# A four-layer graph network on one core: fused maximum, scores through HBM, and a first adjacency matrix turned by TensorE

## The chip, the core and the metric

The kernel runs on one core of a Trainium2 chip. The metric is the device time of one launch, in microseconds (us). A core has engines that work side by side, each through its own queue in order: TensorE (PE in the profile) multiplies matrices and turns 128x128 blocks, and writes to PSUM, eight banks of 128x512 float32; VectorE (DVE) and ScalarE (ACT) work on elements and read PSUM; GpSimd (POOL) works on SBUF; SyncE (SP) issues most of the loads. All data are float32.

## The reference

There are 16 graphs of 1024 nodes with 128 features: x is 16x1024x128, adj is 16x1024x1024 of weights, most of them zero. Four layers follow one another, each on `h = max(layernorm(x), 0)` and added to x:

```python
# layer 0, three times: h = h @ W + b; nh = h / norm(h)
cos = einsum('bij,bkj->bik', nh, nh);  h = einsum('bpq,bqc->bpc', adj * cos, h)
# layer 1
y = maximum((x + einsum('bnf,bnm->bmf', x, adj)) @ W1 + b1, 0) @ W2 + b2
# layer 2: h = x @ W; s1 = h @ a[:f]; s2 = h @ a[f:]
attn = softmax(where(adj > 0, tanh(s1[:, :, None] + s2[:, None, :]), -1e15), -1) @ h
# layer 3: h = x @ W.T + b; e = (h @ A) @ h.T; e = e + e.T
att = softmax(where(adj > 0, e, 0), axis=1) * adj;  h_prime = relu(att @ h)
# then three gates of [x, h_prime], sigmoid and tanh
```

In layer 3 the softmax needs a maximum over 1024 entries for each of the 1024 columns. In layer 2 one score of every node, s1, has to stand in a row that all 128 partitions can read.

## The kernel before

One graph after the other is computed. A graph's nodes are eight blocks of 128; a matrix of 1024x1024 is worked on in eight chunks of 128 rows, each in two halves of 512 columns (`HALVES`). The helpers `pe`, `act`, `dve`, `pool_op` and `op` only record operations, with an estimated duration, the tiles read and written, and a function that emits the instructions. When all 16 graphs are recorded, `Plan.order` (L137) simulates the engines and picks an order: among the operations of the engine that could start first, within `WINDOW`, it takes the one with the lowest rank, which is the graph's due time (`PERIOD` per graph, L345) less the estimated work that still follows it, less an adjustment from the table `LEADS` (L347). The keys of the table name layer, engine and tile; suffixes such as `<0` and `>1` stand for the first two and the last two graphs. `POOLS` and `KINDS` (L338, L339) say how many buffers there are of each kind and how many of them a younger graph may hold. Two further graphs may be under way (`AHEAD`). The instructions are emitted in this order with a manual schedule, so each queue is fixed.

What the change and the prediction touch:

- `load` (L844) loads x of a graph, 512 KB as one DMA on SP's queue; for graph 0 it is two halves. The constants go through `load_const` (L276): the first weights w0 and b0 on ACT's queue, all others on POOL's.
- `turn` (L866) brings the turned adj of a graph, eight tiles adjT of 128x1024. For each there are four DMAs (L879) that put 32x32 squares in their places, in pieces of 32 floats; a 32x32 transpose by DVE (L887) turns the squares, and ACT (L890) copies the tile onto itself to sum its rows (su).
- `layernorm` (L660): statistics on DVE, a power on POOL (L562), then scaling, one half by DVE (L698) and one by ACT (L705). `flipped` (L626) turns the result with TensorE (L569) and evicts it with ACT (`evict`, L622).
- `layer0` (L895): for each chunk, `Square.row` (L748) makes the symmetric product sq: only the upper blocks are multiplied (L760). In most graphs the lower quarter comes back by way of HBM (by_hbm, got), and the rest is turned from copies above (L770, L792). DVE multiplies by adjT (L959) and TensorE accumulates (L822, L833).
- `layer1` loads adj once more, unturned (adjL), and accumulates it with L822.
- `layer2` (L1028): after the projection h, each block's column of scores is widened to 128 columns and turned by TensorE, which leaves the scores in every partition (L1090, eight transposes to a graph); two evictions make s1. Then ACT takes tanh (L1101) and exp (L1105) of each chunk, DVE masks (L1109), TensorE accumulates.
- `layer3` (L1136): for each chunk, DVE masks two halves of the product from PSUM with `adjT > 0` (L1177) into e, reduces 1024 columns to the negated maximum top (L1189); ACT takes exp with that bias and sums (L1193); DVE multiplies by adjT (L1202), and TensorE accumulates.
- The gates follow in `finish` (L1252), and z is stored from ACT's queue.

The heart of layer 3's chunk before the change:

```python
lambda ...: nc.vector.scalar_tensor_tensor(
    by_block(span(e.t, lo, hi), D, 4), by_block(span(aT[j].t, lo, hi), D, 4), 0.0, view(),
    op0=ALU.is_gt, op1=ALU.mult,
),
...
lambda e=e, top=top: nc.vector.tensor_reduce(top.t, e.t[:, 0:N], axis=AX.X, op=ALU.max, negate=True),
```

Of the kernel before, what the change touches and what calls it, by code (L numbers as in the profile page):

```python
# [9 lines left out]
U8 = mybir.dt.uint8  # L10
AF = mybir.ActivationFunctionType
# [3 lines left out]
P = 128  # L15
# [8 lines left out]
FLOOR = 1e-30  # L24

# [197 lines left out]
def tile_adj_preln(  # L223
# [40 lines left out]
    FLAGS = set("CabcdkxhyzTG")  # L264
# [11 lines left out]
    def load_const(group, t, src):  # L276
        def emit():
            with nc.allow_non_contiguous_dma(reason="small parameters, once"):
                (nc.gpsimd if "G" in FLAGS and group is not first else nc.scalar).dma_start(t, src)

        group.append(emit)
# [44 lines left out]
    for load_it in first:  # L326
# [11 lines left out]
    POOLS = {"adjT": 16, "adjL": 5, "x": 3, "big": 13, "above": 2, "got": 1, "bank": 8, "small": 29, "row": 6, "hbm": 3, "hrow": 2}  # L338
    KINDS = {  # L339
        "adjT": ("adjT", 16, 16), "adjL": ("adjL", 5, 5), "x": ("x", 3, 3), "w4": ("big", 12, 8),  # L340
        "chunk": ("big", 11, 4), "above": ("above", 2, 1), "got": ("got", 1, 1), "ps": ("bank", 5, 5),
        "acc": ("bank", 8, 6), "small": ("small", 7, 6), "row": ("row", 3, 3), "hbm": ("hbm", 3, 2),
        "hrow": ("hrow", 2, 1),
    }
    PERIOD, LAST, AHEAD, WINDOW = 60.0, 52.0, 2, 0.05  # L345

    LEADS = {  # L347
        "0 ACT hT": -1, "0 DVE hn": -8, "0 DVE mv": 42.5, "0 DVE nb": -20, "0 DVE st": -77.5, "0 PE ps": -72.5,
        "0 POOL rstd": -1, "00 ACT above": -10.5, "00 ACT hT": 95, "00 ACT hTn": -20.5, "00 ACT sq": -31,
        "00 DMA by": -13.5, "00 DMA got": 15.5, "00 DVE above": -135, "00 DVE ew": 79.5, "00 DVE h": -95.5,  # L350
        "00 DVE ss": -131.5, "00 PE acc0": -252.5, "00 PE ps": -142, "00 PE psP": -0.5, "00 PE sq": -18.5,
        "00 POOL rn": -129.5, "01 ACT above": 56, "01 ACT hT": 11.5, "01 ACT hTn": 15, "01 ACT sq": 15.5,
        "01 DMA by": 4.5, "01 DMA got": 18.5, "01 DVE above": 4.5, "01 DVE ew": 51.5, "01 DVE h": -2.5,
        "01 DVE ss": 16, "01 PE acc0": -164.5, "01 PE ps": 42, "01 PE psP": -5.5, "01 PE sq": -11,
        "02 ACT above": -2, "02 ACT hTn": -615, "02 ACT sq": -25.5, "02 DMA by": 63.5, "02 DMA got": 0.5,
        "02 DVE above": 43.5, "02 DVE ew": -232.5, "02 DVE ss": 79.5, "02 DVE x": -55.5, "02 PE acc0": -28.5,
        "02 PE ps": 12.5, "02 PE sq": 222, "02 POOL rn": -103, "1 ACT g": -33, "1 ACT hn": 66, "1 ACT y1": -7.5,
        "1 DMA adjL": -113, "1 DVE adjL": -21, "1 DVE hn": 1.5, "1 DVE mv": 237.5, "1 DVE nb": 46,
        "1 DVE st": -625.5, "1 DVE x": -0.5, "1 PE acc1": 4, "1 PE py": -167.5, "1 PE py2": 67,
        "1 POOL rstd": -43, "2 ACT e2": -24, "2 ACT h": 287.5, "2 ACT hfl": 53, "2 ACT hn": -13.5,  # L360
        "2 ACT hnT": 18, "2 ACT s1": -14, "2 DVE alone": -51.5, "2 DVE e2": 48.5, "2 DVE h": 20,
        "2 DVE hn": 48.5, "2 DVE hrow": -43.5, "2 DVE mv": -2.5, "2 DVE nb": 78, "2 DVE rden": 9.5,
        "2 DVE x": 10, "2 PE acc2": 108.5, "2 PE p1": -90, "2 PE pf": -26.5, "2 PE ps": 117.5, "2 PE psP": -315,
        "2 POOL rstd": 4.5, "3 ACT above": -19.5, "3 ACT e3": 96.5, "3 ACT gate": -185.5, "3 ACT h3T": 19.5,
        "3 ACT hn": -84.5, "3 ACT hnT": -9.5, "3 ACT hp": -5, "3 ACT hpT": 41, "3 ACT hs": 46.5, "3 ACT z": 25,
        "3 DMA by": -13.5, "3 DMA got": 0.5, "3 DMA z": -130.5, "3 DVE e3": -363.5, "3 DVE gate": 83,
        "3 DVE h": -111.5, "3 DVE hn": 69, "3 DVE mv": -2, "3 DVE nb": 147, "3 DVE st": -192, "3 DVE sum": 53.5,
        "3 DVE top": -84, "3 DVE z": -925, "3 PE acc3": -130.5, "3 PE pg": -18.5, "3 PE ps": 19,
        "3 PE psN": 114, "3 PE psP": 95, "3 PE sq": -0.5, "3 POOL rstd": -59, "3 POOL z": 0.5,
        "T ACT adjT": 1.5, "T DMA adjT": -140.5, "T DVE adjT": -391, "x DMA x": 54.5, "0 ACT hT <0": -2,  # L370
        "0 ACT hT >1": -4.5, "0 ACT hn <1": -4.5, "0 DVE hn <0": 8.5, "0 DVE hn <1": 8.5, "0 DVE hn >0": 15.5,
        "0 DVE hn >1": 1, "0 DVE mv <0": -4.5, "0 DVE mv <1": 113, "0 DVE mv >0": 47.5, "0 DVE mv >1": -25.5,
        "0 DVE nb <0": 101.5, "0 DVE nb <1": -62.5, "0 DVE nb >0": -49, "0 DVE nb >1": -18.5,
        "0 DVE st <0": -85, "0 DVE st <1": -73.5, "0 DVE st >0": -122.5, "0 DVE st >1": -32, "0 PE ps <0": 85.5,
        "0 PE ps <1": 36, "0 PE ps >0": -31, "0 PE ps >1": 40, "0 POOL rstd <0": -6.5, "0 POOL rstd <1": -26,
        "0 POOL rstd >0": -7, "0 POOL rstd >1": 15.5, "00 ACT above <0": -32, "00 ACT above <1": -88,
        "00 ACT above >0": -294, "00 ACT above >1": -3, "00 ACT hT <0": 147.5, "00 ACT hT <1": -7,
        "00 ACT hT >0": 21, "00 ACT hT >1": 161.5, "00 ACT hTn <0": -70.5, "00 ACT hTn <1": 119.5,
        "00 ACT hTn >0": -22, "00 ACT hTn >1": -11, "00 ACT sq <0": -34, "00 ACT sq <1": 134.5,
        "00 ACT sq >0": -119, "00 ACT sq >1": -25.5, "00 DMA by <1": 0, "00 DMA got <1": 1,  # L380
        "00 DVE above <1": -197, "00 DVE ew <0": 180, "00 DVE ew <1": 13, "00 DVE ew >0": -125,
        "00 DVE ew >1": -147.5, "00 DVE h <0": -25.5, "00 DVE h <1": -4.5, "00 DVE h >0": 12,
        "00 DVE h >1": -50.5, "00 DVE params <0": 171, "00 DVE ss <0": 0, "00 DVE ss <1": -73.5,
        "00 DVE ss >0": -46.5, "00 DVE ss >1": -4, "00 PE acc0 <0": -39.5, "00 PE acc0 <1": -212,
        "00 PE acc0 >0": -327.5, "00 PE acc0 >1": -253.5, "00 PE params <0": 56.5, "00 PE ps <0": -18.5,
        "00 PE ps <1": -16, "00 PE ps >0": -32, "00 PE ps >1": -130.5, "00 PE psP <0": -2.5, "00 PE psP <1": 32,
        "00 PE psP >0": -22.5, "00 PE psP >1": -43, "00 PE sq <0": 28.5, "00 PE sq <1": 10, "00 PE sq >0": 3.5,
        "00 PE sq >1": 10, "00 POOL rn <0": -11, "00 POOL rn <1": -164.5, "00 POOL rn >0": -96.5,
        "00 POOL rn >1": -144, "01 ACT above <0": 113, "01 ACT above <1": -11, "01 ACT above >0": 65.5,
        "01 ACT above >1": 24, "01 ACT hT <0": -15, "01 ACT hT <1": -17.5, "01 ACT hT >0": 3.5,  # L390
        "01 ACT hT >1": -39, "01 ACT hTn <0": 16.5, "01 ACT hTn <1": -22, "01 ACT hTn >0": 68,
# [111 lines left out]
    def small(name, n):  # L503
        return Buf("small", [P, n], name)
# [930 lines left out]
```

## Time and profile before

| What | Value |
|---|---|
| median of three runs | 2436.25 us (2435.44 to 2436.89) |
| span of the profiled execution | 2432.9 us |
| granted TensorE clock, mean | 0.996 |
| instructions | 34859 |
| DMA | 263.35 MB, mean 108 GB/s |
| masking in layer 3 from sq, L1177 | 204 of 672 ns; 52 more from got, 681 ns |
| maximum in layer 3, L1189 | 128 of 1212 ns |
| exp with sum in layer 3, L1193 | 128 of 1149 ns, and 187 ns to read the sum |
| score transposes, L1090 | 128 of 273 ns each as recorded |
| stream transposes of adjT, L887 | 128 of 1224 ns |
| copies of adjT with sum, L890 | 128 of 1055 ns, and 190 ns to read the sum |

A page of the profile gives, for one execution, each engine's busy time; then 40 equal slices of the span with busy tenths; then groups of instructions. A group's line names the source line, engine and operation, what it writes and reads, and the tile shapes; then the number of instructions, the busy time with the mean duration of one in ns, and the engine's idle time before them with what ended it. Matmuls are pipelined: a recorded duration holds the way through the array, and what one costs in a stream is read from the distance of the starts. A float32 matmul is recorded as two instructions, a transpose as one.

The idle time of an engine is told by windows of time (busy us of each engine in each stretch), and the timeline shows instructions in order, with the idle time in front and what ended it.

### The profile page before, as it was taken

The numbers are of one execution on the slowest core, as the hardware profiler recorded it, in microseconds if no ns is written. First come the engines' busy times: TensorE is split into PE (matmuls) and PEld (weight loads), VectorE is DVE, ScalarE is ACT, GpSimd is POOL, SyncE is SP. The second block draws the span as 40 slices with busy tenths as digits, with TensorE's granted clock in tenths as the row PEclk, the third lists the DMA queues.
The fourth block names the chain that finished last, engine by engine and source line by source line (L and its number), as shares of the span: only waits on it lengthen the run. The fifth ranks groups of instructions, "written<-read, shape, count | busy, mean of one in ns | idle before, by whom it ended". The sixth has DMA issues, their size and how long they took to land. (4 is left out here: it accounts for less than half of the span.)

```text
span 2432.9 us, 34859 instructions
## 1 busy us (share of the span) xinstructions
PE 2387.8 (98%) x11946; PEld 1589.5 (65%) x11946; DVE 2107.7 (87%) x5264; ACT 1288.8 (53%) x2404; POOL 245.1 (10%) x166
## 2 busy tenths in 40 slices
PE   6999999999999999999999999999999999999996
PEld 3568576675767657676675767757576675765763
DVE  6758989889998988999888998998999888897676
ACT  5316564645646465554744646455454644656275
POOL 3001010100101101010010101001011010100011
PEclk9999999999999999999999999999999999999998
DMA  9531927549295573936639285473936738063000
GB/s 149 111 104 36 173 53 148 130 88 171 62 165 121 103 155 81 166 86 136 142 80 180 53 164 130 92 151 80 165 103 122 155 75 151 18 94 89 27 1 18
DMA packets 1126321, 263.35 MB, mean 108 GB/s; under 512 B 970016, under 2 KB 1109552, under 8 KB 1126144
## 3 DMA queue, kind: packets, MB, share of 16 engines
q1 hardware_dynamic: 1108368, 251.73, 52.9%
q10 hardware_dynamic: 16944, 8.52, 1.2%
q8 instruction: 94, 1.54, 0.3%
q0 software_dynamic: 832, 0.88, 0.3%
q14 instruction: 83, 0.68, 0.1%
HBM read 198.14 MB, written 62.91 MB: 107 GB/s over the span
## 5 line engine op out<-in xcount | busy, mean ns | idle before, releaser
L959 DVE SCALAR_TENSOR_TENSOR ew<-sq,rn,adjT 128x512 f32<-128x512 f32 x612 | 432.3, 739 | 83.3 <-ACT above L792 45.6
L822 PE MATMUL acc<-ew,h 128*128 128x512 f32 x1024 | 477.9, 593 | 2.1 <-DVE ew L959 2.1
L760 PE MATMUL sq<-hTn 128*128 128x512 f32 (+3 forms) x1152 | 432.8, 488 | 0.7 <-DVE above L782 0.4
L792 ACT COPY above<-sq 128x256 f32<-128x256 f32 (+3 forms) x432 | 168.2, 394 | 448.5 <-PE sq L760 248.7
L760 PEld LDWEIGHTS sq<-hTn 128*128 128x128 f32 x1152 | 201.4, 192 | 155.2 <-issue 103.9
L822 PEld LDWEIGHTS acc<-ew,h 128*128 128x128 f32 x1024 | 178.9, 190 | 161.8 <-issue 124.0
L833 PEld LDWEIGHTS acc<-h,ew 128*128 128x128 f32 x2048 | 240.8, 192 | 22.6 <-issue 18.8
L833 PE MATMUL acc<-h,ew 128*128 128x128 f32 x2048 | 250.3, 276 | 0.0
L822 PE MATMUL acc<-e,hs 128*128 128x512 f32 x512 | 242.1, 597 | 5.3 <-DVE e L1202 4.1
L833 PEld LDWEIGHTS acc<-h,e 128*128 128x128 f32 x2048 | 232.9, 192 | 11.9 <-issue 6.5
L833 PE MATMUL acc<-h,e 128*128 128x129 f32 x2048 | 233.8, 275 | 1.2 <-DVE e L1109 1.2
L822 PE MATMUL acc<-adjL,hn 128*128 128x512 f32 x512 | 233.5, 593 | 0.3 <-ACT hn L726 0.3
L562 POOL TENSOR_TENSOR rstd<-ve,mhalf 128x8 f32<-128x8 f32 x64 | 105.2, 1643 | 1237.1 <-DVE ve L681 1237.1
L1193 ACT ACTIVATE e<-e,top 128x1024 f32<-128x1024 f32 x128 | 147.0, 1149 | 133.8 <-DVE top L1189 131.8
L770 PEld LDWEIGHTS sq<-ident,above 128*128 128x128 f32 x960 | 125.7, 141 | 125.6 <-issue 89.0
L890 ACT ACTIVATE adjT<-adjT 128x1024 f32<-128x1024 f32 x128 | 135.0, 1055 | 137.2 <-DVE adjT L887 94.5
L770 PE MATMUL sq<-ident,above 128*128 128x128 f32 x960 | 175.1, 273 | 2.0 <-ACT above L792 2.0
L705 ACT ACTIVATE hn<-x,nb,rstd 128x128 f32<-128x128 f32 x256 | 105.3, 482 | 122.8 <-DVE nb L689 115.2
L1109 DVE SCALAR_TENSOR_TENSOR e<-adjT,e 128x512 f32<-128x512 f32 x256 | 158.8, 681 | 9.3 <-ACT e L1105 8.7
L887 DVE STREAM_TRANSPOSE adjT<-adjT 128x1024 f32<-128x1024 f32 x128 | 154.7, 1224 | 11.7 <-DMA adjT<-in_adj_dram 11.0
L782 DVE STREAM_TRANSPOSE above<-sq 128x512 f32<-128x512 f32 x208 | 146.5, 707 | 17.2 <-PE sq L760 17.1
L1202 DVE TENSOR_TENSOR e<-e,adjT 128x512 f32<-128x512 f32 x248 | 161.2, 681 | 0.0
(149 smaller groups left out, 3512.0 us busy)
## 6 DMA issues: line engine op xcount, KB each, us to landing
adjT<-in_adj_dram SPq DMA_DIRECT2D x512, 128.0 KB, 4.0
adjL<-in_adj_dram SPq DMA_DIRECT2D x128, 512.0 KB, 5.0
by_hbm<-above SPq DMA_DIRECT2D x104, 512.0 KB, 3.7
got<-by_hbm SPq DMA_DIRECT2D x416, 128.0 KB, 3.0
x<-in_x_dram SPq DMA_DIRECT2D x15, 512.0 KB, 4.6
out_dram<-z ACTq DMA_DIRECT2D x15, 512.0 KB, 5.6
x<-in_x_dram SPq DMA_DIRECT2D x2, 256.0 KB, 4.9
out_dram<-z ACTq DMA_DIRECT2D x2, 256.0 KB, 2.2
```

What stands on the lines that cost most here:

```text
L760: lambda: nc.tensor.matmul(dst.t[:, (first - lo) * P :], cols(leftT.t, j), span(rightT.t, first, hi), start=True, stop=True),
L770: nc.tensor.transpose(cols(dst.t, r), cols(above.t, p), ident)
L782: lambda: nc.vector.transpose(span(above.t, p, p + 4), read.t),
L792: lambda: nc.scalar.copy(span(above.t, p, p + hi - first), read.t[:, (first - lo) * P :]),
L822: lambda s=s, lo=lo, hi=hi: nc.tensor.matmul(acc[s].t, cols(h.t, at, w), span(ew.t, lo, hi), start=(j == 0), stop=(j == NB - 1)),
L833: nc.tensor.matmul(a.t[:, (c - lo) * n : (c - lo + 1) * n], cols(ew.t, c), h.t[:, at * w : at * w + n], start=(j == 0 and c == lo), stop=( ...
L887: dve(V(N), [t], [t], lambda t=t: nc.vector.transpose(t.t, t.t), True)
L890: lambda t=t, c=c: nc.scalar.activation(t.t, t.t, AF.Copy, accum_out=su.t[:, c : c + 1]),
L959: lambda view=view, ew=ew, rn=rn, j=j, lo=lo, hi=hi: nc.vector.scalar_tensor_tensor(by_block(span(ew.t, lo, hi), D, 4), view(), rn.t[:, j ...
L1109: lambda e=e, j=j, lo=lo, hi=hi: nc.vector.scalar_tensor_tensor(span(e.t, lo, hi), span(aT[j].t, lo, hi), 0.0, span(e.t, lo, hi), op0=ALU. ...
L1193: lambda e=e, top=top, tot=tot: nc.scalar.activation(e.t[:, 0:N], e.t[:, 0:N], AF.Exp, bias=top.t, accum_out=tot.t),
L1202: lambda e=e, j=j, lo=lo, hi=hi: nc.vector.tensor_mul(span(e.t, lo, hi), span(e.t, lo, hi), span(aT[j].t, lo, hi)),
```

## The change

Four flags are switched on, and the plan's tables are replaced.

- `m`: in layer 3, ACT makes a mask of 0 and 1 in int8 from each adjT tile by Sign and then Relu, in one of five new buffers. DVE multiplies the mask by the product and takes the maximum of the half in the same instruction; a small reduction joins the two maxima and negates.
- `r`: in layer 2 of every graph but the last, one transpose turns the 128x8 scores into 8x128, ACT evicts it, a DMA writes it to HBM, and a second DMA reads it back into all 128 partitions as s1. The last graph keeps the eight transposes.
- `H`: for graph 0, adj comes in eight blocks of 128 columns (pieces of 512 bytes, buffers of kind adjL); TensorE turns them, eight transposes to a block, and ACT evicts the halves with their sums.
- `W`: the second half of x of graph 0, and x of graphs 1 and 2, are issued on ACT's queue, the latter two after the second eviction of graph 0's first hT; from graph 2 on, the loads of x are kept in order; all constants are loaded from POOL's queue.
- `POOLS`, `KINDS`, `PERIOD`, `LAST` and every entry of `LEADS` are new, so all queues are ordered anew. The top and sum columns get a pool of their own, `dot`.

```diff
-    FLAGS = set("CabcdkxhyzTG")
+    FLAGS = set("CabcdkxhyzTGmrHW")
...
-                (nc.gpsimd if "G" in FLAGS and group is not first else nc.scalar).dma_start(t, src)
+                (nc.gpsimd if "W" in FLAGS or "G" in FLAGS and group is not first else nc.scalar).dma_start(t, src)
...
-        "adjT": ("adjT", 16, 16), "adjL": ("adjL", 5, 5), "x": ("x", 3, 3), "w4": ("big", 12, 8),
-        "chunk": ("big", 11, 4), "above": ("above", 2, 1), "got": ("got", 1, 1), "ps": ("bank", 5, 5),
-        "acc": ("bank", 8, 6), "small": ("small", 7, 6), "row": ("row", 3, 3), "hbm": ("hbm", 3, 2),
-        "hrow": ("hrow", 2, 1),
+        "adjT": ("adjT", 16, 16), "adjL": ("adjL", 5, 5), "x": ("x", 3, 3), "w4": ("big", 9, 10),
+        "chunk": ("big", 11, 4), "above": ("above", 2, 1), "got": ("got", 1, 1), "ps": ("bank", 6, 8),
+        "acc": ("bank", 8, 8), "small": ("small", 8, 9), "row": ("row", 3, 2), "hbm": ("hbm", 3, 3),
+        "hrow": ("hrow", 1, 2), "mask": ("mask", 5, 5), "dot": ("dot", 8, 5),
     }
-    PERIOD, LAST, AHEAD, WINDOW = 60.0, 52.0, 2, 0.05
+    PERIOD, LAST, AHEAD, WINDOW = 59, 45.5, 2, 0.05
...
         for lo, hi in HALVES if "x" in FLAGS and b == 0 else ((0, NB),):
+            queue = nc.scalar if "W" in FLAGS and (b == 0 and lo or b in (1, 2)) else nc.sync
...
+            if "W" in FLAGS and b > 1:
+                plan.place_after(o, loads["x"])
+            loads["x"] = o
+            if "W" in FLAGS and b in (1, 2):
+                plan.place_after(o, [p for p in plan.ops if p.key == "0 ACT hT"][1])
+                o.preds.add([p for p in plan.ops if p.key == "0 ACT hT"][1])
...
+        for c in range(NB) if sh else ():
+            t = Buf("adjT", [P, N], f"adjT_{b}_{c}")
+            raw = Buf("adjL", [P, N], f"raw_{b}_{c}")
+
+            def plain(raw=raw, c=c):
+                nc.sync.dma_start(by_block(raw.t), adj[b].rearrange("(a p) j -> p a j", p=P)[:, :, c * P : (c + 1) * P])
+
+            o = op("DMA", 1.9, [], [raw], plain)
...
+            for s, (lo, hi) in enumerate(HALVES):
+                p = ps(f"raw_{b}_{c}_{s}")
+                flip(raw, lo, hi, p)
+                evict(p, t, lo, hi, accum=(sh, 2 * c + s))
...
+        if "r" in FLAGS and b < B - 1:
+            pt, sr = ps(f"pt_{b}"), rowbuf(f"sr_{b}")
+            pe(
+                TR, [h], [pt],
+                lambda: nc.tensor.transpose(pt.t[0:NB, 0:P], by_block(h.t, E2)[:, :, D], ident),
+            )
+            act(S(P), [pt], [sr], lambda: nc.scalar.copy(sr.t[0:NB], pt.t[0:NB, 0:P]))
+            sd = Buf("hrow", [NB, P], f"sd_{b}")
+            op("DMA", 0.2, [sr], [sd], lambda: nc.sync.dma_start(sd.t, sr.t[0:NB]), lat=2.2)
+            op(
+                "DMA", 1.8, [sd], [s1],
+                lambda: nc.sync.dma_start(s1.t[:, 0:N], sd.t.rearrange("c p -> (c p)").partition_broadcast(P)),
+                lat=2.4,
+            )
...
+            if "m" in FLAGS:
+                mask = Buf("mask", [P, N], f"mask_{b}_{j}")
+                act(
+                    S(N), [aT[j]], [mask],
+                    lambda mask=mask, j=j: nc.scalar.activation(mask.t, aT[j].t, AF.Sign),
+                )
+                act(S(N), [mask], [mask], lambda mask=mask: nc.scalar.activation(mask.t, mask.t, AF.Relu))
+                peak = dot(f"peak_{b}_{j}", 2)
...
+                if "m" in FLAGS:
+                    dve(
+                        V(HALF) + 0.06, [blk(mask, lo, hi), p], [blk(e, lo, hi), blk(peak, s, s + 1, 1)],
+                        lambda e=e, view=view, mask=mask, peak=peak, s=s, lo=lo, hi=hi: nc.vector.tensor_tensor_reduce(
+                            by_block(span(e.t, lo, hi), D, 4), by_block(span(mask.t, lo, hi), D, 4), view(), 1.0, LOWEST,
+                            op0=ALU.mult, op1=ALU.max, accum_out=peak.t[:, s : s + 1],
+                        ),
+                        p is square.got,
+                    )
...
-            top = small(f"top_{b}_{j}", 1)
-            tot = small(f"sum_{b}_{j}", 1)
-            dve(
+            tot = dot(f"sum_{b}_{j}", 1)
+            if "m" in FLAGS:
+                dve(
+                    TINY, [peak], [top],
+                    lambda peak=peak, top=top: nc.vector.tensor_reduce(
+                        top.t, peak.t, axis=AX.X, op=ALU.max, negate=True
+                    ),
+                )
```

## The prediction, made before the changed kernel was run

> **What bounds the kernel now.** I read the busy shares first, then the slices, then the windows, because a share over the whole span hides where the idle time lies.
>
> ```profile
> PE 2387.8 (98%) x11946; PEld 1589.5 (65%) x11946; DVE 2107.7 (87%) x5264; ACT 1288.8 (53%) x2404; POOL 245.1 (10%) x166
> ```
> ```profile
> PE   6999999999999999999999999999999999999996
> DVE  6758989889998988999888998998999888897676
> ACT  5316564645646465554744646455454644656275
> ```
> ```profile
> 0.00:60.00 60.00, 39.82 (x158) 23.88 (x159) 39.66 (x106) 30.16 (x60) 23.11 (x36) 0.95 1.10 149
> ...
> 500.00:650.00 150.00, 150.00 (x740) 98.76 (x739) 134.31 (x339) 77.79 (x145) 13.36 (x8) 1.00 0.61 120
> ...
> 2300.00:2433.00 133.00, 110.56 (x512) 69.54 (x510) 97.69 (x268) 80.88 (x151) 25.12 (x12) 0.95 0.07 20
> ```
>
> In the windows the columns after the length are PE, weight loads, DVE, ACT and POOL busy, then clock, DMA share and GB/s. TensorE is idle for 2432.9 - 2387.8 = 45.1 us, and 20.2 of them lie in the first 60 us, 22.4 in the last 133. Between, it never rests, at clock 1.00. A busy TensorE need not be a full one, so I checked its spacing in the timeline of TensorE alone:
>
> ```profile
> 2300.46 11.32 PE L822 MATMUL acc<-adjL,hn 128*128 128x512 f32 x26
> 2311.62 0.60 PE L569 MATMUL ps_hnT<-ident,hn 128*128 128x128 f32 x4
> ...
> 2338.20 0.60 PE L1090 MATMUL p<-ident,h 128*128 128x128 f32 x4
> 2338.64 1.04 PE L770 MATMUL sq<-ident,above 128*128 128x128 f32 x8
> ```
>
> 26 matmuls start in 2311.62 - 2300.46 = 11.16 us, 0.429 us each, and that is also the usual spacing elsewhere: the stream has no bubbles. Four transposes take 0.44 us, 0.110 each. So in the middle only less work on TensorE buys time. DVE (134.3 of 150 us) and ACT (77.8) follow it; relief on DVE buys nothing there. At the two ends other things decide:
>
> ```profile
> 2.34 38.50 SPq L879 DMA_DIRECT2D adjT<-in_adj_dram  x32
> ...
> 7.82 0.87 DVE L670 BATCH_NORM_STATS2 st<-x 128x6 f32<-128x128 f32 x4 [2.85 <-DMA x<-in_x_dram]
> ...
> 12.53 2.01 PE L569 MATMUL ps_hT<-ident,hn 128*128 128x128 f32 x8 [12.53 <-DVE hn L698]
> ...
> 40.42 1.25 DVE L887 STREAM_TRANSPOSE adjT<-adjT 128x1024 f32<-128x1024 f32 x1 [2.40 <-DMA adjT<-in_adj_dram]
> ```
> ```profile
> 2390.64 1.13 DVE top L1189
> 2391.77 1.19 DVE e L1177 x2
> 2392.96 1.13 DVE top L1189
> 2394.16 1.18 DVE e L1177 x2
> 2395.34 1.13 DVE top L1189
> ```
>
> At the start, TensorE waits 12.5 us for the first layer norm, whose second half of x comes at 7.8, and the first graph's turned adj trickles in until 44.5 us (32 DMAs, 38.5 / 32 = 1.2 us apart). At the end the chain of waits alternates on DVE between masking and the maximum of layer 3.
>
> **What the Trainium skill says.** "TensorE: Matmul & The Clock Gate", Part 1: after about 3.4 us of idleness the array falls to half clock. The trace agrees: after the 4.9 us of idleness before 55.65 us, the clock over 56 to 62 us is 0.56. "ScalarE: Activation LUTs", Table sets: cheap functions ride in every set, and another set costs about 2.66 us. The trace has one table load (1283 ns) although exp, tanh, relu and square alternate; the page does not list Sign for this set. "VectorE: DVE Perf Modes", Two Vector instructions with no wait between them: an op that writes its accumulator is two instructions, the second reading it out. No DVE op here has one; ACT's read-out takes 187 ns. "DMA: Bandwidth & Descriptors", Issuing engines are not separate DMA queues: a second issuing queue saves issue time alone.
>
> **The change part by part.** Durations are of the profiled execution, whose span is 2432.9 us; the median 2436.25 is 3.4 above it. I apply the difference to the median.
>
> *Scores through HBM.* For graphs 0 to 14, eight transposes (L1090) become one: 15 x 7 x 0.110 = 11.5 us off TensorE, in its saturated stretch: worth 11.5 us. Two evictions into s1 (618 ns) become one of 128 columns (about 270 ns as hfl, L1067). In exchange two DMAs on SP's queue. The nearest rows are by_hbm (3.7 us to landing) and got (3.0), so the first tanh of layer 2 comes some 6 us later than by transposes. While it does, TensorE has other graphs' matmuls, since two batches ahead may run. If that cover failed, each graph would lose up to 6 us, 15 x 6 = 90; I take 0. On SP the write waits for the eviction, and adjT, adjL, by_hbm, got and x loads queue behind it; adjT has a whole graph of buffers and adjL five, so a wait of a few us there is covered. The added bytes are 15 x 0.5 MB on 263 MB.
>
> *Fused maximum.* Per chunk the reduction of 1024 (1212 ns) goes. Two maskings from adjT (672 ns) become two multiplications with an accumulator, and a tiny maximum of two columns (150 ns as the reciprocal) is added. The read-out is not in this trace: I bound it between 0.06 us (about the step of the tiniest DVE ops) and 0.19 (ACT's), and take 0.1. DVE per graph: 8 x (1.21 - 0.15 - 2 x 0.1) = 6.9 us less. In the middle that is worth nothing; DVE goes from 134 to about 127 of 150. ACT gets Sign and Relu over 1024 elements per chunk, 16 x 1.05 = 16.8 us a graph (as exp without bias, L1105, 1052 ns), so about 94 of 150. Each of these is a 1.05 us block in front of the evictions that TensorE's banks wait for. They depend on adjT alone, with five mask buffers, so they can be early; ACT has 72 us of slack per 150. Bounds: 0 and 0.2 us of TensorE stall per instruction (256 x 0.2 = 51 us); I take 0.01, that is 2 us. In the tail the maximum is on the chain: 8 x (1.13 - 0.35) = 6.2 us could go, but the last three chunks' masks, beyond the five buffers, add 6.3 us to ACT, which has about 21 us of work in those 33 us (8 exps of 1.34 with read-out, 8 hs of 0.40, above, gate). I take 5 of 6.2, with 0 and 7 as bounds.
>
> *First adj in column blocks.* 32 DMAs of 128-byte pieces become eight of 512-byte ones. The x load of the same size and piece issues in 0.72 us and lands in 4.6. Their 4.2 MB at 200 GB/s (an estimate, somewhat above the busiest slice's 180) take 21 us, so the last lands near 24 us instead of 44; the 9.9 us of stream transposes (8 x 1.24) leave DVE. Added are 64 transposes: 64 x 0.110 = 7.0 us of TensorE and 16 evictions with read-out, 16 x 0.79 = 12.6 us of ACT in place of 8 x 1.24 = 9.9. The transposes need no layer norm, so they fill part of the idle start and the gaps of the first convolution. The idleness before 55.65 (4.9 us, then half clock, about 2 us more) follows from the late adj: the hT eviction sits on ACT behind an adjT copy. It should go, since graph 1's adj also begins 20 us sooner. What is late next is the first layer norm and the chain of convolutions.
>
> *First x on two queues, constants on POOL.* x's second half starts with the first half, though beside adj's packets: I estimate 5.5 us instead of 7.8, so the first useful matmul near 10.3 (bounds 9.5 and 12.5). w0 and b0 move from ACT to POOL, whose loads here take 5 us to land: there by 8, needed after 11. x of graphs 1 and 2 waits for the first hT eviction; only ACT's queue stands behind that, at a time when it must wait anyway.
> Start: before it costs 20.2 us of idleness and about 4 of half clock. After, about 9 before the first instruction (the first MB, x of graphs 0 and 1, is there by 9.6 now; then it will be x and the first adj tile), 2 of clock, 4 of small gaps and 7.0 of transposes: 22. Worth 2, and some 2 more from 60 to 130 us, where graph 1 is no longer late: 4, bounds -3 and 9.
>
> *New order, pool sizes and due times.* In the middle there is nothing left to win (idleness is 0 from 500 to 2300 us); at the tail the 22.4 us of idleness include about 11 after the last accumulation, which stay. I take 2 us of gain there, bounds -5 and 6.
>
> Sum: 11.5 - 2 + 5 + 4 + 2 = 20.5, so 2436.25 - 20.5 = 2415.8, about **2416 us**.
>
> **Rivals.** *Only TensorE's own sum counts* (the ends give nothing): 11.5 - 7.0 = 4.5, 2432 us. For it: both ends are chains, which a new link can lengthen again. Against: the late adj is plainly a transfer.
> *The ends give all*: start 9, tail 7 + 6, stalls 0: 33.5, 2403 us. For it: DVE leads the chain at the end. Against: ACT is busy there too.
> *Slower: the masks hold up ACT.* 256 instructions of 1.05 us before evictions, on an engine that works in order; TensorE has at most six transient banks. The gain before this cost is 22.5 us, so it decides from 22.5 / 256 = 0.09 us of TensorE stall per mask instruction; at 0.2 us the time is 2436.25 - 22.5 + 51 = 2465. For it: ACT's evictions ended waits of TensorE at the start. Against: in the middle ACT waits for TensorE (248.7 us for sq), not the reverse.
> *Sign lies in another table set*: two switches a chunk, 128 x 2 x 2.66 = 681 us more on ACT, which then has 2250 us of work and gaps in it; some 2650 us. One load in the trace and the page's wording speak against it.
>
> **How the numbers follow.** Forecast 0.64, all to the ends 0.13, TensorE's sum alone 0.10, masks 0.11, table 0.02. This kernel's measurement tells no less than about 0.2%, that is 4.9 us, from no change. Forecast and second case are faster; of the third, 0.04 is faster and 0.06 within 0.2%; the last two are slower: 0.81, 0.06, 0.13. The range of 2400 to 2433 leaves out the slower cases and some 0.06 below.
>
> **What would show it.** TensorE: 11946 - 105 + 64 = 11905 matmuls, busy all of each middle window at clock 1.00; anything below 149 of 150 there is the mask rival. DVE's masking rows near 0.67 us with a short read-out; two ACT groups x128 near 1.05 us and a single table load. The eighth adj tile evicted before 27 us, the first layer norm's transpose near 10 us, no gap near 55. In the tail no 1.13 us pieces of the maximum in the chain. I am wrong if the middle gets bubbles, or if the start ends later in spite of the earlier adj.

## The result, and the profile after

The changed kernel takes 2432.57 us in the median (2430.06 to 2435.09, 20 runs), the kernel before, measured beside it, 2435.51. One of the 20 runs of the kernel before took 8522.44 us; without it the median is 2435.44. The ratio is 0.9988, with a 95% interval of 0.9981 to 0.9994: faster by about 3 us, where 20 were forecast. The profiled execution of the changed kernel has a span of 2429.9 us (2432.9 before).

The busy times of the page after:

```profile
PE 2393.4 (98%) x11905; PEld 1588.7 (65%) x11905; DVE 1979.3 (81%) x5513; ACT 1504.5 (62%) x2661; POOL 246.7 (10%) x168
```

Busy times by stretch, changed kernel: window, its length, then PE, PEld, DVE, ACT, POOL with counts, the clock, the DMA share and GB/s:

```profile
0.00:60.00 60.00, 51.63 (x240) 34.20 (x241) 42.19 (x115) 43.23 (x92) 24.12 (x38) 1.00 1.09 192
500.00:650.00 150.00, 150.00 (x759) 100.37 (x757) 128.10 (x353) 95.71 (x169) 13.32 (x8) 1.00 0.68 123
```

The new work, by line, in the changed kernel: count, then total and mean ns of one:

```profile
L1260 DVE CUSTOM_DVE_ANT_0 e<-mask,sq 128x512 f32<-128x512 int8 x204 | 135.2, 676 | 18.0 <-ACT above L821 11.2 <-PE sq L799 4.6
L1249 ACT ACTIVATE mask<-adjT 128x1024 int8<-128x1024 f32 x128 | 134.9, 1056 | 5.8 <-DVE peak L1260 5.8
...
L1260 DVE DVE_READ_ACCUMULATOR2_ANT peak<- 128x1 f32 x256 | 21.0, 82 | 0.0
L1281 DVE TENSOR_REDUCE top<-peak 128x1 f32<-128x2 f32 x128 | 18.0, 143 | 0.8
```

Every instruction came out near the price the forecast gave it: 11905 matmuls, VectorE at 128 of 150 us, ScalarE at 96, masking still 0.68 us, a read-out of 82 ns, masks of 1.06 us. What is off isn't in these lines; it has to be in how the parts stand to one another.

The middle window is also a trap. PE is busy 150.00 of 150 us, as before the change. The end of a matmul is modelled in these records: a transpose's lasts 0.27 us, and the next one starts 0.109 us after it, so gaps below some 0.16 us vanish in the busy time. So for the account below TensorE's waits are taken from the start times: from one matmul or transpose to the next, less the spacing of the same form back to back (0.429 us for 512 columns, 0.112 for 128, 0.109 for a transpose). What a lower clock adds to the spacing counts as a wait too. With the spacings as rounded here, the middle column reads some 3 us lower and the own work as much higher in both kernels; the differences stay. One row is one profiled execution, in us; before the first instruction counts to the start, and the last column is what follows TensorE's last instruction:

| kernel | TensorE's own work | to 100 | 100 to 2300 | 2300 to 2380 | 2380 to its last | after it |
|---|---|---|---|---|---|---|
| before | 2363.1 | 29.1 | 10.1 | 7.9 | 11.8 | 10.9 |
| changed | 2358.6 | 17.4 | 19.4 | 17.3 | 6.1 | 11.2 |
| difference | -4.5 | -11.7 | +9.3 | +9.3 | -5.7 | +0.3 |

The start gave what was expected, and so did the last 50 us, where the maximum had been in the chain. But 9.3 us came back in the middle and 9.3 between 2300 and 2380 us. The experiments look for these two.

**Where the middle waits.** The added waits lie mainly at one place in a graph: layer 0's second product, where the projection psP goes through VectorE (h), TensorE (ps_hTn) and ScalarE (hTn) before the first sq can start. I call it the hand-over. Of the waits above 30 ns between 350 and 1960 us (12.1 us in the changed kernel), 5.2 stand between the transposes of ps_hTn, 1.9 between them and the first sq, and 2.7 between the first sq, in part for the second half of hTn; the kernel before has 3.0 us in all, and none there. Here is TensorE's timeline there, kernel before (start, length, line, operation; a matmul is two records, a transpose is one):

```profile
1047.45 1.05 PE L600 MATMUL psP<-w,hT 128*128 128x128 f32 x8
...
1194.17 1.05 PE L600 MATMUL psP<-w,hT 128*128 128x128 f32 x8
1195.06 0.83 PE L600 MATMUL psP<-w2e,hnT 128*128 128x130 f32 x6
1195.73 1.05 PE L600 MATMUL psP<-w,hT 128*128 128x128 f32 x8
1196.63 0.83 PE L600 MATMUL psP<-w2e,hnT 128*128 128x130 f32 x6
1197.30 0.60 PE L569 MATMUL ps_hTn<-ident,h 128*128 128x128 f32 x4
1197.73 0.61 PE L600 MATMUL psP<-w2e,hnT 128*128 128x130 f32 x4
1198.18 0.60 PE L569 MATMUL ps_hTn<-ident,h 128*128 128x128 f32 x4
1198.62 0.39 PE L1064 MATMUL pf<-w2f,hrow 128*128 128x128 f32 x2
1198.84 1.04 PE L1090 MATMUL p<-ident,h 128*128 128x128 f32 x8
1199.72 3.39 PE L760 MATMUL sq<-hTn 128*128 128x512 f32 x8
```

The same place in the changed kernel:

```profile
1042.42 2.01 PE L629 MATMUL psP<-w,hT 128*128 128x128 f32 x16
...
1189.10 2.01 PE L629 MATMUL psP<-w,hT 128*128 128x128 f32 x16
1190.94 0.39 PE L1123 MATMUL pf<-w2f,hrow 128*128 128x128 f32 x2
1191.17 1.57 PE L598 MATMUL ps_hTn<-ident,h 128*128 128x128 f32 x8
1192.70 2.78 PE L789 MATMUL sq<-hTn 128*128 128x512 f32 x6
```

Before, layer 2 of the graph ahead (psP from w2e, pf, and the eight score transposes p of L1090) stands between the pieces of the hand-over and hides its two latencies. After, the new order has sent layer 2's products ahead, and seven of the eight score transposes are gone; only pf is left. The eight transposes of ps_hTn take 1.53 us to the first sq where eight back to back take 0.87. And from one graph to the next it is 1194.17 - 1047.45 = 146.72 us before and 1189.10 - 1042.42 = 146.68 after, although 0.77 us of transposes left each graph.

### The profile page after: what moved, and what is told of

Read it like the earlier page. It is cut to its first block, busy times and chain, and to the rows that moved or that the text cites. A ratio compares the mean times of both kernels' runs of the same rounds, so it can differ in the third digit from the quotient of the medians.

```text
span 2429.9 us, 35227 instructions
## 1 busy us (share of the span) xinstructions
PE 2393.4 (98%) x11905; PEld 1588.7 (65%) x11905; DVE 1979.3 (81%) x5513; ACT 1504.5 (62%) x2661; POOL 246.7 (10%) x168
## 4 chain that ended last, share of the span: by engine, by line
PE 92%; SPq 2%; DVE 2%; DMA 2%; ACT 2%; issue 0%; POOLq 0%; POOL 0%; DVEq 0%; ACTq 0%
PE acc L851 34%; PE sq L789 19%; PE acc L862 18%; PE psP L629 5%; PE sq L799 4%; PE py L1080 2%; PE py L639 2%; PE ps_hTn L598 2%; SPq L938 2%; PE psN L629 1%; PE pg L639 1%; PE ps_hnT L598 1%; DMA by_hbm<-above 1%; DMA got<-by_hbm 1%; PE ps_hT L598 1%; SPq L842 0%
## 5 line engine op out<-in xcount | busy, mean ns | idle before, releaser
L949 ACT ACTIVATE adjT<-adjT 128x1024 f32<-128x1024 f32 x120 | 126.6, 1055 | 101.8 <-DVE adjT L946 96.7
L946 DVE STREAM_TRANSPOSE adjT<-adjT 128x1024 f32<-128x1024 f32 x120 | 144.1, 1220 | 19.7 <-DMA adjT<-in_adj_dram 18.7
L851 PEld LDWEIGHTS acc<-adjL,hn 128*128 128x128 f32 x512 | 93.2, 190 | 101.1 <-issue 87.4
L851 PEld LDWEIGHTS acc<-e,hs 128*128 128x128 f32 x512 | 91.0, 192 | 93.9 <-issue 79.3
```

What stands on the lines that cost most here:

```text
L851: lambda s=s, lo=lo, hi=hi: nc.tensor.matmul(acc[s].t, cols(h.t, at, w), span(ew.t, lo, hi), start=(j == 0), stop=(j == NB - 1)),
L946: dve(V(N), [t], [t], lambda t=t: nc.vector.transpose(t.t, t.t), True)
L949: lambda t=t, c=c: nc.scalar.activation(t.t, t.t, AF.Copy, accum_out=su.t[:, c : c + 1]),
```

## Experiments: the middle

Theory A: the score transposes were pure load on TensorE, as the forecast took them. Theory B: they stood in the hand-over and hid a wait that is now bare. Theory C: the masks on ScalarE delay the evictions (the forecast's slower rival). All runs keep the planner's order, unless told otherwise; only what an operation emits is changed. Times are medians, with the kernel before at 2435.3 to 2436.3 us on the same chips.

**The kernel before with fewer score transposes** (`b_few_scores`):

```diff
-                for c in range(lo, hi):
+                for c in range(lo, lo + 1 if b < B - 1 else hi):
                     at = c * E2 + D
                     nc.tensor.transpose(cols(p1.t, c - lo), h.t[:, at : at + 1].to_broadcast([P, P]), ident)
...
```

> The kernel before, its order of instructions kept, with one score transpose in place of four for each half of graphs 0 to 14 (the eviction spreads that one block of 128 scores over its half, so the scores of the other blocks are left out). TensorE has 6 x 15 = 90 transposes of 0.109 us less, 9.8 us. Theory A (TensorE's sum is the bound, what is taken from it shows): about 2425.7 us against 2435.5, ratio 0.996. Theory B (the score transposes stood in the hand-over of layer 0's second product, between ps_hTn and the first sq, and hid the eviction of hTn there; without them TensorE waits): at most 2 us of the 9.8 are gained, 2433.5 to 2435.5, and the trace has a new gap of about 0.6 us a graph between ps_hTn and sq. Theory C (the masks on ScalarE cost the time in the middle of the changed kernel): this kernel has no masks, so it gains the 9.8 as in A.

2434.79 us, ratio 0.9996 (0.9988 to 1.0004): of 9.8 us of transposes at most 3 show, and none is certain. Its timeline:

```profile
1047.29 1.05 PE L600 MATMUL psP<-w,hT 128*128 128x128 f32 x8
...
1193.99 1.05 PE L600 MATMUL psP<-w,hT 128*128 128x128 f32 x8
...
1198.66 0.38 PE L1090 MATMUL p<-ident,h 128*128 128x128 f32 x2
1199.13 3.49 PE L760 MATMUL sq<-hTn 128*128 128x512 f32 x8
1202.82 0.33 PE L770 MATMUL sq<-ident,above 128*128 128x128 f32 x1 [0.21 <-ACT above L792]
```

The first sq starts 0.41 us sooner after psP (5.14 us against 5.55), but the first mirrored block waits for ScalarE, and comes 8.83 us after psP, as before (1203.01 - 1194.17 = 8.84). The period is 146.70. In the middle the waits rose from 10.1 to 19.0 us, by 8.9 of the 9.8. That is B, in a kernel with no part of the change in it; only the place is a little later than I had said, behind the first sq as well as ahead of it. A falls. C, for which this kernel without masks should have gained all of the 9.8, falls with it.

**More transposes in the changed kernel**, at three places: behind pt, behind pf, and inside ps_hTn (`a_more_at_pt`, `a_more_at_pf`, `a_more_in_gap`):

```diff
-                lambda: nc.tensor.transpose(pt.t[0:NB, 0:P], by_block(h.t, E2)[:, :, D], ident),
+                lambda: [
+                    nc.tensor.transpose(pt.t[0:NB, 0:P], by_block(h.t, E2)[:, :, D], ident) for _ in range(8)
+                ],
...
-            lambda: nc.tensor.matmul(pf.t[:, 0:D], hrow.t, w2f, start=True, stop=True),
+            lambda: [nc.tensor.matmul(pf.t[:, 0:D], hrow.t, w2f, start=True, stop=True)] + [
+                nc.tensor.transpose(pf.t[:, D : 2 * D], hrow.t, ident) for _ in range(7 if b < B - 1 else 0)
+            ],
...
             for c in range(lo, hi):
+                if dst.name in [f"ps_hTn_{b}_1_1" for b in range(2, B - 2)]:
+                    nc.tensor.transpose(cols(dst.t, c - lo), cols(src.t, 0, w), ident)
                 nc.tensor.transpose(cols(dst.t, c - lo), cols(src.t, c, w), ident)
```

> The changed kernel, its order kept, with the one score transpose pt of a graph done eight times over: 7 x 15 = 105 transposes of 0.109 us more on TensorE, 11.4 us, in the middle of running acc matmuls. A and B both: the whole 11.4 us shows, about 2444 us (ratio to the kernel before 1.0035), since TensorE doesn't wait at that place. If a bound other than TensorE set the period of a graph at 146.85 us, less than half of it shows, under 2438.

> The changed kernel, its order kept, with the same 105 transposes of 0.109 us more, but 7 a graph right behind pf, which in most graphs is the last work ahead of the two halves of ps_hTn that wait for VectorE's h. A (sum): 2444 us as in the run with them at pt. B (TensorE stands idle there for about 1 us in a graph anyway): most of the 11.4 us vanishes in the gaps, 2433 to 2437 us, and the waits inside ps_hTn are gone from the trace.

> The changed kernel, its order kept, with 4 transposes of 0.109 us more in each of graphs 2 to 13 (48 in all, 5.2 us on TensorE), this time one ahead of each of the four transposes of ps_hTn's second half in layer 0's second product, where TensorE waits about 0.13 us for each block of VectorE's h. A (the sum): the 5.2 us show, about 2437.5 us, as the 11.4 us did at pt. B (the time given back is TensorE waiting for h at this place, free for other work): under 1.5 us show, 2432 to 2434 us, and the waits inside ps_hTn fall from about 0.5 to under 0.2 us a graph.

At pt: 2443.31 us, 10.7 more than the changed kernel. At that place TensorE is the bound. At pf: 2445.03, no better; A's number, against B. But the waits did not stay where they were. The timeline of this run:

```profile
1198.41 0.93 PE L1124 MATMUL pf<-ident,hrow 128*128 128x128 f32 x7
1199.17 1.04 PE L598 MATMUL ps_hTn<-ident,h 128*128 128x128 f32 x8
1200.71 2.77 PE L789 MATMUL sq<-hTn 128*128 128x512 f32 x6 [0.50 <-ACT hTn L651]
```

The eight transposes of ps_hTn now run back to back, as B said, yet a wait of 0.50 us for ScalarE's hTn has taken the place. ScalarE's queue has pf's eviction (1199.37) ahead of a square (1199.53) and the first hTn (1200.07), so what lengthens pf lengthens the hand-over. Between 350 and 1960 us the waits inside ps_hTn fall from 5.2 to 0.7, and those ahead of the first sq rise from 1.9 to 6.7. That expectation of B overlooked the queue. Inside ps_hTn nothing stands behind the added transposes but the wait itself, and there it costs nothing: 2431.72 us (0.9983, 0.9977 to 0.9990), the changed kernel's time within the interval, with 48 transposes more. The timeline of that run:

```profile
1193.08 0.60 PE L600 MATMUL ps_hTn<-ident,h 128*128 128x128 f32 x4
1193.51 0.27 PE L599 MATMUL ps_hTn<-ident,h 128*128 128x128 f32 x1
1193.62 0.27 PE L600 MATMUL ps_hTn<-ident,h 128*128 128x128 f32 x1
...
1194.33 0.31 PE L600 MATMUL ps_hTn<-ident,h 128*128 128x128 f32 x1
1194.61 2.78 PE L791 MATMUL sq<-hTn 128*128 128x512 f32 x6
```

Twelve transposes from 1193.08 to 1194.61, 1.53 us; the changed kernel takes the same 1.53 us for eight. So the waits inside ps_hTn, about half of what was added at the hand-over, are TensorE keeping step with VectorE's h, and they are free for other work. The other half, behind ps_hTn, is in the main for ScalarE's hTn; no run fills it by itself.

**Narrow masks** (`a_narrow_masks`):

```diff
-                    lambda mask=mask, j=j: nc.scalar.activation(mask.t, aT[j].t, AF.Sign),
+                    lambda mask=mask, j=j: nc.scalar.activation(mask.t[:, 0:P], aT[j].t[:, 0:P], AF.Sign),
...
-                act(S(N), [mask], [mask], lambda mask=mask: nc.scalar.activation(mask.t, mask.t, AF.Relu))
+                act(S(N), [mask], [mask], lambda mask=mask: nc.scalar.activation(mask.t[:, 0:P], mask.t[:, 0:P], AF.Relu))
```

> The changed kernel, its order kept, with Sign and Relu of the mask over 128 columns in place of 1024; the reduce takes this block for all eight, so seven eighths of the mask are left out. ScalarE loses 256 x about 0.75 us = 190 us of work. C (the masks on ScalarE delay the evictions that TensorE waits for): the middle falls by most of its 9 us of added waits, 2421 to 2424 us, and the waits inside ps_hTn shrink. B: the middle doesn't move, for the hand-over waits for VectorE's h and the layer's own eviction. At the end (from 2300 us): if ScalarE's load with masks is what cost 3.9 us there, 4 to 10 us come off, 2423 to 2429; if the new order cost it, less than 2 us, 2431 to 2433.

2429.66 us (0.9971, 0.9961 to 0.9982). The middle didn't move: 20.0 us of waits against 19.4. C falls. After 2300 us the waits fell from 23.4 to 20.1 (by 1.1 up to 2380 us, by 2.3 after): ScalarE's masks cost the end some 3 us, between my two expectations.

## Experiments: the maximum and the end

**The maximum by itself**, short in the kernel before, and as before in the changed kernel, for the last two graphs or for all (`b_short_max`, `a_old_max_at_end`, `a_old_max`):

```diff
-                lambda e=e, top=top: nc.vector.tensor_reduce(top.t, e.t[:, 0:N], axis=AX.X, op=ALU.max, negate=True),
+                lambda e=e, top=top: nc.vector.tensor_reduce(top.t, e.t[:, 0:P], axis=AX.X, op=ALU.max, negate=True),
...
-                    lambda mask=mask, j=j: nc.scalar.activation(mask.t, aT[j].t, AF.Sign),
+                    lambda mask=mask, j=j: b >= B - 2 or nc.scalar.activation(mask.t, aT[j].t, AF.Sign),
...
```

> The kernel before, its order kept, with the maximum ahead of layer 3's exponential taken over 128 columns in place of 1024 (the rest is left out). VectorE loses 128 x about 0.93 us, 119 us, and nothing goes to ScalarE: the most that a cheaper maximum can give without a new order. Theory D (what the forecast took for the end is there to be had): 4 to 7 us, all of it after 2300 us, about 2430 us. Theory E (at the end other links of the chain carry the time): under 2 us, 2434 to 2436 us. In the middle both expect nothing.

> The changed kernel, its order kept, with the last two graphs' maximum taken as before: no Sign and Relu there (32 ScalarE instructions of 1.05 us less), e masked without the accumulator and reduced over its 1024 columns (16 VectorE instructions of about 1.06 us in place of 0.14). If the masks' load on ScalarE cost the end more than the fused maximum gave it: 1 to 4 us less, 2428.5 to 2431.5. If the fused maximum gains at the end what the forecast said, 3 to 7 us more, 2435 to 2440.

> The same for all graphs: the changed kernel in its order, without any masks on ScalarE and with the maximum as before. What the fused maximum is worth in this order, by itself. If VectorE's load bounds nothing in the middle (TensorE does, with the waits at its hand-over): the same as the run with the last two graphs changed, within 2 us. If VectorE's 118 us of added reductions push the middle: the waits of TensorE between 100 and 2300 us grow from 19 to over 25 us and the time goes over 2440 us.

A short maximum makes the kernel before 6.3 us faster (2429.79; 0.9973, 0.9963 to 0.9983), and TensorE's waits after 2380 us fall from 11.8 to 5.9: theory D, the size the forecast gave it. Taking the fused maximum away from the last two graphs makes the changed kernel slower, 2438.63 us (1.0011, 1.0004 to 1.0017), 6 us above the changed kernel. So at the end the masks' 3 us are already paid out of a gain, and the fused maximum is worth some 6 us net in this order. Without it in all graphs the changed kernel's order takes 2489.06 us, and the waits in the middle go from 19 to 70: this order leans on the lighter VectorE. That isn't the worth of the fused maximum by itself, for the order of the kernel before lives with the longer one.

If the maximum gave what it should, the 9.3 us between 2300 and 2380 us are of another cause. Busy times of this stretch, and TensorE's timeline between the last graph's score transposes p and its accumulation acc, kernel before:

```profile
2300.00:2380.00 80.00, 75.17 (x388) 50.77 (x387) 60.83 (x189) 54.22 (x100) 16.89 (x9) 0.99 0.06 21
...
2339.51 1.02 PE L760 MATMUL sq<-h3T,gT 128*128 128x512 f32 x2
...
2341.57 3.60 PE L822 MATMUL acc<-e,hs 128*128 128x512 f32 x8
...
2348.52 1.61 PE L833 MATMUL acc<-h,e 128*128 128x129 f32 x12 [1.20 <-DVE e L1109]
```

Changed kernel, and then its TensorE timeline where the longest wait stands:

```profile
2300.00:2380.00 80.00, 69.75 (x366) 48.79 (x365) 48.45 (x170) 63.24 (x100) 10.07 (x5) 0.91 0.02 7
```

```profile
2327.64 0.76 PE L1163 MATMUL p<-ident,h 128*128 128x128 f32 x5 [0.32 <-ACT h L1109]
2328.23 0.39 PE L1123 MATMUL pf<-w2f,hrow 128*128 128x128 f32 x2
2333.84 16.61 PE L862 MATMUL acc<-h,e 128*128 128x129 f32 x128 [5.22 <-DVE e L1182]
2350.28 0.60 PE L789 MATMUL sq<-h3T,gT 128*128 128x256 f32 x2
```

Layer 2 of the last graph waits 5.22 us for its first e. There is work left: of graph 14's layer 3, 16 of 24 records of the product and all 32 of the accumulation are still to come. But TensorE's queue has them behind the 128 records of the last graph's acc, from 2350.28 on. Before, these products and the first 8 records of the accumulation stood between p and acc, and the wait was 1.20 us. The clock falls with it, 0.99 to 0.91 over the window: it was 0.65 from 2334 to 2340 us, and the 128 records take 16.44 us where 0.112 each makes 14.3. By the starts the wait is 5.4 us against 1.4, so this one place makes some 6 of the 9.3 us. With narrow masks the wait is still 4.47 us, so it isn't the masks'.

**Order alone.** The instructions and buffers stay, the sequence of each engine is moved about (`a_reordered`, `b_reordered`):

```diff
     ordered = plan.order()
+    ordered = [ordered[i + a] for i, a in enumerate(SHIFTS)]
```

> The changed kernel with the same instructions and buffers in another order: each engine's sequence was moved about, instruction by instruction, from the gaps of TensorE in the planner's own timetable, as long as its dependences allow it. The timetable loses 11.4 us: 1 at the start, 3 in the middle, 7 after 2300 us; the hand-over of layer 0's second product keeps its gap, for layer 2's products have all gone ahead of it. Expected: 2420 to 2424 us, the gap inside ps_hTn still there (F: the gap comes from what stands ahead of it, not from the search that made the order). If the order at the end was not what cost 9 us between 2300 and 2380 us, less than 3 us are gained, over 2429.

> The kernel before, none of the change in it, its instructions and buffers moved about in the same way and for as long. The timetable loses 22.8 us: 5 at the start, 12 in the middle, 5 after 2300 us; TensorE's gaps in the middle fall to 3 us, since layer 2's products and score transposes can fill the hand-over. F: 2414 to 2420 us, below the changed kernel treated alike, so that the change's parts are worth less than the order around them. If the parts themselves carry the gain: above the changed kernel treated alike by 3 us or more.

The kernel before, with none of the change, takes 2419.14 us in the new order (0.9931, 0.9917 to 0.9944); the changed kernel 2418.55 (0.9925, 0.9912 to 0.9937). By order alone the two gain 17 and 14 us, five to six times what the whole change gained; the second lies 1.5 us below its expected range. Between the two there is no difference that can be measured, so neither F's "below" nor the rival's 3 us above is right. But F's reason shows in the waits between 100 and 2300 us: 5.7 us in `b_reordered`, 15.8 in `a_reordered`, where the hand-over is still bare. Of the 14 us of `a_reordered`, 8.7 come after 2300 us, yet not from the longest wait there: layer 2 of the last graph still waits 5.77 us for e, with graph 14's layer 3 behind it. `b_reordered` has no such wait.

**Layer 2's products back in the hand-over** (`a_filled`), with new due times and a new `LEADS`, and `a_filled_slack`, the same with later transfers assumed when the sequences were worked out:

```diff
+    for b in range(2, 13):
+        turned = [o for o in plan.ops if o.key == "01 PE psP" and o.batch == b + 1][0]
+        plan.place_after([o for o in plan.ops if o.key == "2 PE psP" and o.batch == b][1], turned)
     ordered = plan.order()
+    ordered = [ordered[i + a] for i, a in enumerate(SHIFTS)]
...
```

> The changed kernel's instructions (fused maximum, scores through HBM, first adj in column blocks, first x on two queues) with new due times, and with one rule more: in graphs 2 to 12 the second of layer 2's three psP groups may not start before the next graph's first psP half of layer 0's second product. So layer 2's products stand in that hand-over again, as in the kernel before, and the one score transpose goes after them; then moved about instruction by instruction as the other two reordered kernels. The timetable has 3.5 us of gaps between 100 and 2000 us (12 in the reordered kernel that lacks this rule) and ends 22.7 us sooner than the changed kernel's. Theory G (the score saving is real and was given back only because layer 2's products had been moved away from the hand-over): 2406 to 2412 us, TensorE's waits in the middle at 5 us or less, and 7 us or more below both other reordered kernels. If the round trip through HBM costs TensorE time wherever it is put: no better than the reordered kernel without the rule, 2418 us.

> The kernel with layer 2's products back in the hand-over, its hand-over order on TensorE unchanged, and everything else moved about once more with later transfers in the timetable: the mirrored squares (got) 1.8 us later, the scores (s) 0.5 and the adj tiles 1.0, since in the run before it VectorE waited 19.4 us for got between 350 and 1960 us and TensorE for its masks. The timetable ends 1.8 us later than that run's. G (the score saving can be had, once nothing stands bare and no transfer is late): TensorE's waits between 100 and 2300 us fall from 19.7 to under 9, 2406 to 2411 us, clearly below the 2418.6 and 2419.1 of the two reordered kernels. H (the round trip's time comes back as a wait wherever the work is put): 2416 to 2420 us, and waits for s or for layer 2's e in place of those for got.

The first missed: 2419.57 us. The hand-over was filled and its waits were gone, but 19.7 us of waits stood in the middle all the same, at irregular places. VectorE's waits for transfers between 350 and 1960 us (total, times, longest), in this run:

```profile
DVE ew L1236 <- DMA got<-by_hbm: 19.4, 13, 3.8
```

and in the changed kernel:

```profile
DVE ew L1018 <- DMA got<-by_hbm: 2.9, 4, 1.1
```

I read it so: an order as tight as this one has no room for a mirrored square that lands late; VectorE stops for it, and e for layer 2 stands behind it in the queue. Of TensorE's waits above 150 ns between 100 and 2300 us, 4.6 us are for that e. With room for late transfers the second run takes **2403.98 us** (0.9872, 0.9855 to 0.9888), the fastest of all. Its busy times and hand-over:

```profile
PE 2373.9 (99%) x11905; PEld 1585.9 (66%) x11905; DVE 1982.3 (83%) x5513; ACT 1502.6 (63%) x2661; POOL 247.3 (10%) x168
```

```profile
1034.51 1.05 PE L855 MATMUL psP<-w,hT 128*128 128x128 f32 x8
...
1180.12 1.05 PE L855 MATMUL psP<-w,hT 128*128 128x128 f32 x8
1181.01 0.61 PE L855 MATMUL psP<-w2e,hnT 128*128 128x130 f32 x4
1181.45 1.05 PE L855 MATMUL psP<-w,hT 128*128 128x128 f32 x8
1182.35 0.83 PE L855 MATMUL psP<-w2e,hnT 128*128 128x130 f32 x6
1183.02 0.60 PE L824 MATMUL ps_hTn<-ident,h 128*128 128x128 f32 x4
1183.45 0.39 PE L1349 MATMUL pf<-w2f,hrow 128*128 128x128 f32 x2
1183.76 0.28 PE L1358 MATMUL pt<-ident,h 128*8 128x128 f32 x1
...
```

The period is 1180.12 - 1034.51 = 145.61 us, 1.1 below the kernel before: the 0.77 us of transposes, and some of the waits that were there before. From 100 to 2300 us TensorE waits 7.6 us in place of 19.4. At the end, graph 14's layer 3 again covers the last graph's layer 2 (the 5.22 us are gone):

```profile
2323.79 1.06 PE L1389 MATMUL p<-ident,h 128*128 128x128 f32 x8
2324.69 6.17 PE L1077 MATMUL acc<-e,hs 128*128 128x512 f32 x14
2330.70 0.38 PE L1349 MATMUL pf<-w2f,hrow 128*128 128x128 f32 x2
2330.92 14.30 PE L1088 MATMUL acc<-h,e 128*128 128x129 f32 x121
```

So G holds, with a time 2 us below its range, and H falls: TensorE's wait for layer 2's e goes from 4.6 to 0.5 us and VectorE's for got from 19.4 to 6.7, while ScalarE's waits for s stay as they were (9.7 after 10.3 us). The saved score work can be had, with the round trip through HBM in place. Filling the hand-over gave nothing without room for the transfers (2419.57 against 2418.55); the room without the filling was not run. How the 31 us below the kernel before divide between the parts of the change and the order stays open too, since the kernel before was not given the new due times and the assumed slack.

## Why the prediction was wrong

Two of its terms failed, the scores through HBM and the new order at the tail. The others came out near their size.

- *TensorE's own work*: -11.5 for the transposes and +7.0 for the first adj were right (-4.5 measured), and so was the count of 11905.
- *Start*: -4 was right in sum. Waits to 100 us fell by 11.7, less 7.0 of added transposes, -4.7. The first layer norm's transpose starts at 10.2 us, the gap at 55 is gone. Only the eighth adj tile was later than I said, evicted at 33 us and not before 27. No run separates the column blocks from the second queue.
- *Fused maximum at the end*: 5 us of gain, masks included. A short maximum without masks gives 6.3, and the fused one in the last two graphs 6. Right in mechanism and about in size. That relief on VectorE buys nothing in the middle held for the old order, where the short maximum took 1.2 us off the waits there, and not for the new one, as `a_old_max` shows.
- *Masks in the middle*: +2. Narrow masks moved nothing there; 0 within what can be seen.
- *Scores through HBM* is the first step that failed: "worth 11.5 us", since the transposes lay in TensorE's "saturated stretch", with the round trip covered by other graphs' matmuls, "I take 0". The round trip itself was covered (ScalarE waited 1.0 us in all for s between 350 and 1960 us). But the transposes, and layer 2's products, which the new order sent ahead, were themselves the cover of another wait. The term is 11.5 less 9.3, about 2 us. `b_few_scores` and `a_more_in_gap` show this from both sides, and `a_filled_slack` that it isn't the fault of the round trip. The 90 us that I had set as a bound were for the latency of the transfer, and none was set for the place that the removed work leaves.
- *New order at the tail* is the second, and in time the larger: 2 us of gain, bounds -5 and 6. In the trace the stretch from 2300 to 2380 us lost 9.3, outside the bounds. That most of it is the order's and not the masks' rests on the narrow masks, which take 1.1 us off this stretch, and on `a_filled_slack`: it has the same instructions, the same masks among them, with graph 14's layer 3 ahead of the last graph's acc, and no wait there. No run moved that work alone, so that the one place costs some 6 of the 9.3 us is read from the trace only.
- The test that I named, "anything below 149 of 150", could not have shown the bubbles: both windows read 150.00.
- The work that the table-set rival gives ScalarE, 2250 us, adds up to about 2240 (1289 + 269 + 681). Nothing rests on it.

-4.7 at the start, -11.45 + 9.3 in the middle and +3.9 after 2300 us make the 3 us. The forecast had -4, -9.5 and -7. The rival "only TensorE's own sum counts" named 2432 us, and is right by accident: its reason, that the ends give nothing, is not what happened.

## What to carry to other kernels

On a bound engine, ask of an instruction that you remove what it hides: list what stands between its neighbours in the trace, and which latency of theirs ends behind it. Work is worth its length only where the engine doesn't wait when it is gone, and the cheapest test is to put dummy work into the suspected gap, where nothing else is queued behind it. When several parts come with a new order, judge the order as a part of its own, for here it went both ways: the new one took back much of what the parts gave, and moving instructions about, with nothing else changed, gave 14 and 17 us.

## What the runs showed that was not expected

- Busy times of TensorE hide waits: 150.00 of 150 us with about 0.2 to 0.4 us (before) and 1.0 to 1.1 us (changed) of waits in it, seen only from start times.
- An order fitted to tight transfer times lost 15.6 us to one with 0.5 to 1.8 us of room for each transfer (2419.57 against 2403.98), though its own timetable was the shorter by 1.8.
- VectorE multiplies an int8 mask with a PSUM tile, keeps the maximum, and takes 676 ns for 128x512; the read-out of the accumulator takes 82 ns. Sign, Relu, Exp and Tanh alternated on ScalarE with one table load.
